# First element of a graph kernel: earlier x, later bias columns, row loads on two queues, weight sums and one row combination moved

## Chip, cores and metric

The kernel runs on one core of one Trainium2 chip. The metric is the device time of one execution in microseconds (us). Lower is better.

## The reference

There are 16 independent elements. Each has node features `x` (1024 x 128) and a dense adjacency matrix `adj` (1024 x 1024), all in float32. An element passes through two stages, each followed by a residual and a layer norm:

```python
# stage 0
degree = adj.sum(-1)[:, :, None]
agg = einsum('bid,bij->bjd', x, adj) / degree
x = layernorm(x + relu(concat([x, agg], -1) @ W.T + b))
# stage 1: four layers
def layer(nodes, adj, ws, bs, wd, bd, wn, bn, wu, bu):
    src = einsum('bjv,bij->biv', nodes @ ws + bs, l2norm(adj, rows))
    dst = einsum('bjv,bji->biv', nodes @ wd + bd, l2norm(adj, columns))
    return tanh(concat([src, nodes @ wn + bn, dst], 2) @ wu + bu)
# layers three and four also see the inputs of earlier layers
x = layernorm(x + layer4(layer3(layer2(layer1(x)))))
```

So each layer multiplies the messages once with the column-normalised adjacency and once with the row-normalised one. These products are nearly all of the work.

## The kernel before

**Tiling.** The 1024 nodes are eight blocks of 128. `a` holds the adjacency of one element in eight blocks of rows (4 MB), `at` its transpose in two halves. Halves of the 1024 columns are written `h` = 0 and 1, and half 1 is worked on first. From layer two on, the two aggregations are done by a seven-product (Winograd) scheme: `y` and `yt` name the four quadrants of `a` and of `at`, `combine_1` overwrites one quadrant by a difference (L672), and `combine(2..4)` build the combinations `T` of `a` and `Q` of `at` (L676, L678, L680; one takes 2.28 us on VectorE). Layer one of the first element is plain (`plain_layer`, L849), because its combinations are not there yet.

**Order.** The order is written out by hand. Each engine executes its instructions in the order of the program text, and a queue issues its DMAs in that order as well. SP (`nc.sync`) carries nearly all DMAs; GpSimd (POOL) issues some at the start. Work of VectorE, ScalarE and GpSimd beside an aggregation is put in by `hooks`: a dictionary from the index of a TensorE step to the function that is called just before that step is issued. Elements after the first have most of their preparation done during the element ahead of them. The first element has no such cover, so it has its own opening, L1045 to L1256.

**The opening.** `load_nodes(q, h)` (L1057) loads half `h` of `x` in four DMAs of 64 KB. `load_pair(q, i, groups)` (L1052) loads two row blocks of the adjacency; SP and POOL carry half of each pair, 256 KB per DMA. `to_xT(h)` transposes a half of `x` on TensorE (L1094) and copies it out on ScalarE (L1095). `weights_of_x(h)` multiplies it by the first half of W (L1179). For each pair, `squares_of` makes the squares of its rows on ScalarE (L1139) and the degrees on VectorE (L1145), and `gathers_of` multiplies `x` by the rows on TensorE (L1152). `add_square(i)` adds the squares of a block into one sum on GpSimd (L1142). `degree_inverses` (L1149) and `degree_row` (L357, L1172) turn the degrees into a row that scales the gathered sums, `scaled` (L1175); then come `weights_of_agT` (L1182), `with_x` (L1190, L1192), the layer norm (L468 to L488) and `to_x1` (L1197). `root_inverses` (L373, L374) takes inverse roots of the sums of squares on VectorE and GpSimd.

**Weights and biases.** `fetch_weights` (L187, L189) loads a layer's weights, `load_biases(i, q)` (L1079) one bias vector per DMA: 9 for i = 0, 8 for i = 1. `bias_columns(i)` transposes them on TensorE (L1084) and copies them on ScalarE (L1085, L1087). `fold_begin` and `fold_end` (L203 to L228) multiply the layers' weight matrices into one. `sums_of_weights` and `weight_sums` (L148 to L155) build the sums of the folded weights that the seven-product scheme needs.

**Rows.** The transpose `at` is made from a second reading of the adjacency by rows, in four groups `rows[0..3]` of 1 MB; a group is eight DMAs of 128 KB (`load_rows_piece`, L638). ScalarE scales them by the row norms (`scale_rows`, L645), VectorE transposes them in blocks of 32 (`transpose_rows`, L653).

Of the kernel before, what the change touches and what calls it, by code (L numbers as in the profile page):

```python
# [14 lines left out]
P = 128  # L15
NL = 4
CHUNKS = [1, 1, 2, 3]
G = 4
# [5 lines left out]
def adj_resnorm_kernel(ctx: ExitStack, tc: tile.TileContext, x, adj, w0, b0, layers, out):  # L24
# [33 lines left out]
    nc = tc.nc  # L58
# [5 lines left out]
    C = P // G  # L64
# [561 lines left out]
    def load_rows(b, q, st):  # L626


        n = QB // len(st)
        for i, piece in enumerate(st):  # L630
            load_rows_piece(b, q, piece, i * n, n)
        return st

    def load_rows_piece(b, q, piece, k, n):
        v = adj[b, q * QB * C:(q + 1) * QB * C].rearrange("(k r) (h g j) -> h g r k j", r=C, h=NH, g=G)
        for g in range(G):
            for h in range(NH):
                nc.sync.dma_start(piece[g * C:(g + 1) * C, :, h * P:(h + 1) * P], v[h, g, :, k:k + n])  # L638
        return piece

    def scale_rows(st, q, rinv, which=range(QB)):
# [424 lines left out]
    for i in range(4):  # L1066
        load_pair(nc.sync, i, (0, 1))
        load_pair(nc.gpsimd, i, (2, 3))
        if i == 1:
            load_nodes(nc.gpsimd, 0)  # L1070
    biases_of = [[b0, *layers[0][1::2], *layers[1][1::2]], [*layers[2][1::2], *layers[3][1::2]]]
    in_rows = one.tile([P, HW], F32, tag="S3", name="biases")
# [4 lines left out]
    def load_biases(i, q, s=slice(None)):  # L1077
        for k, v in list(enumerate(biases_of[i]))[s]:
            q.dma_start(in_rows[k:k + 1, i * P:(i + 1) * P], v.rearrange("(o p) -> o p", o=1))  # L1079
# [11 lines left out]
    def to_xT(h):  # L1091
        pt = small(f"xtr0_{h}", [HW])
        for q in range(BPH):
            nc.tensor.transpose(pt[:, q * P:(q + 1) * P], xn[:, h * BPH + q], ident)  # L1094
        nc.scalar.copy(nodes(xT[:, half(h)]), blocks(pt))  # L1095
# [12 lines left out]
    places[1] = one.tile([P, 2 * NJ, HW // 2], F32, tag="T2", name="rows1_0")  # L1108
    rows, fetched = {}, []
    for l, q in enumerate((None, None, 2, 3)):  # L1110
        if l in (1, 2):
            load_biases(l - 1, nc.sync)
        fetched.append(fetch_weights(raw, l, nc.sync, bcs[l], None if l else wm))
        if q is not None:
            rows[q] = load_rows(0, q, [places[q]])
    wm = as_chunks(wm, 0)
    for q in (0, 1):
        rows[q] = load_rows(0, q, [places[q]])
# [22 lines left out]
    def add_square(i):  # L1141
        nc.gpsimd.tensor_add(sq[4], sq[4], sq[i])  # L1142
# [8 lines left out]
    def gather(h, i):  # L1151
        nc.tensor.matmul(pa[h], xn[:, i], a[:, i, half(h)], start=(i == BPH), stop=(i == BPH - 1))  # L1152

    def squares_of(h, k):
        for i in range(h * BPH + k, h * BPH + k + 2):
            square(i)
            degree(i)
# [19 lines left out]
    def weights_of_x(h):  # L1177
        pw[h] = product(f"pw0_0_{h}")
        nc.tensor.matmul(pw[h], w0T[:, 0], xT[:, half(h)], start=True, stop=False)  # L1179
# [14 lines left out]
    def to_x1(h):  # L1194
# [2 lines left out]
            nc.tensor.transpose(pt[:, q * P:(q + 1) * P], x1n[:, h * BPH + q], ident)  # L1197
        nc.scalar.copy(x1T[:, half(h)], pt)

    weights_of_x(1)  # L1200
    squares_of(*PAIRS[0])
    gathers_of(*PAIRS[0])
    squares_of(*PAIRS[1])
    gathers_of(*PAIRS[1])
    to_xT(0)
    weights_of_x(0)
    nc.vector.tensor_add(sq[6], sq[6], sq[7])
    add_square(5)
    add_square(6)
# [1 line left out]
    degree_row(1)  # L1211
    squares_of(*PAIRS[2])
    gathers_of(*PAIRS[2])
    bias_columns(0)
    add_square(0)
    add_square(1)
    first, second = 2, 3
    nc.scalar.activation(sq[second], a[:, second, :], AF.Copy, accum_out=cols[:, 2 * NB + second:2 * NB + second + 1])
    degree(first)
    gather(1, first)  # L1220
    gather(1, second)
    degree_inverses(0)
    degree_row(0)
    scaled(1)
# [1 line left out]
    weights_of_agT(1)  # L1226
    square(first)
    gather(0, second)
    add_square(first)
    scaled(0)  # L1230
    with_x(1)
    weights_of_agT(0)
# [4 lines left out]
    fold_end(0, fetched[0])  # L1237
    stats[0] = norm_stats(pn[0], range(BPH), "0_0_0")
    root_inverses(cols, inv, slice(NB))
    add_square(second)  # L1240
    biases = fold_begin(1, fetched[1], nc.vector.tensor_copy, True)
    for q in range(BPH):
# [18 lines left out]
    for b in range(B):  # L1261
# [8 lines left out]
        if b == 0:  # L1270
            def row_factors0():
                column_sums(0, st0)
                for q in (2, 3):
                    scale_rows(rows[q], q, rinv)

            def second_x1():
                to_x1(0)
                bias_columns(1)
                fold_begin(2, fetched[2])
                ahead["spread"] = row_inverses(0, inv)  # L1280

            def factors_and_fold():
                nonlocal rinv
                fold_end(2, fetched[2])
                rinv = gather_inverses(0, ahead["spread"])

            ahead = {}
            t = messages(b, 0, feats, wm, {0: second_x1, 1: factors_and_fold, 2: row_factors0}, with_sums=False)
            cinv = {}

            def columns0(rows, h, engine=nc.vector):
                scale_columns(a, cinv[0], rows, half(h), engine)

            def rows0(destination, finish):
                for q in (2, 3):
                    transpose_rows(rows[q], q, at)
                sums_of_weights(2, fetched[2][3])
                weight_sums(own_seven(2, fetched[2][3]))
                nc.sync.dma_start(wsave[2], fetched[2][3])

            def cinv0(destination, finish):
                cinv[0] = factor_rows_now(0, 1, inv, "cinv")

            def second0(destination, finish):
                columns0(range(NJ, NB), 1)
                destination(1, cinv[0])
                columns0(range(NJ), 1)

            def fold_and_scale(l, q):
                fold_begin(l, fetched[l])  # L1310
                scale_rows(rows[q], q, rinv)

            def first0(destination, finish):
                columns0(range(NJ, NB), 0, nc.gpsimd)
                columns0(range(2), 0, nc.gpsimd)
                for q in (0, 1):
                    transpose_rows(rows[q], q, at)
                destination(0, cinv[0])
                columns0(range(2, NJ), 0)

            def sums0(destination, finish):
                combine_1(y)
                finish(1)
                combine(2, y, T)
                combine_1(yt)
                combine(3, y, T)

            def folded(l, part):
                return lambda *_: part(l, fetched[l])

            hooks = {4: lambda *_: inverses(0, st0, NB), 6: rows0, 7: cinv0,
                     9: lambda *_: fold_and_scale(3, 0), 11: second0, 12: folded(3, fold_end),
                     14: lambda *_: scale_rows(rows[1], 1, rinv), 18: first0, 26: sums0}
            T = combined(0, "T")
            plain_layer(b, 0, feats, t, wm, a, at, f1, "acc", hooks)
            wm = message_weights(b, 1)
            a2 = load(n)
            xs2 = load_spread(n)
        else:
            w = {}  # L1340
            if nxt:
                st = begin_sums(n)
            t = messages(b, 0, feats, wm)
            if nxt:
                w["a"] = load(n)
            Q = combined(b, "Q")
            ahead = {}

            def weights1(ahead=ahead):
                combine(4, y, T)  # L1350
                ahead["wm"] = message_weights(b, 1)

            def rows3():
                transpose_rows(rows[0], 0, at)

            def sums1(w=w, st=st):
                if nxt:
                    for i in range(2):
                        squares_of_row(n, w["a"], st, i)

            def additions(*which, then=(), w=w, st=st):
                def issue():
                    if nxt:
                        for i in which:
                            add_squares(n, st, i)
                        for i in then:
                            squares_of_row(n, w["a"], st, i)
                return issue

            hooks = {0: rows3, 3: weights1, 5: lambda: combine_1(yt), 7: lambda: combine(2, yt, Q),  # L1370
                     9: lambda: combine(3, yt, Q), 15: sums1, 16: additions(1), 17: lambda: combine(4, yt, Q),
                     18: additions(then=(2, 3)), 23: additions(2), 27: additions(3)}
            aggregate(b, 0, feats, t, wm, a, at, T, Q, f1, "row", hooks)
            wm = ahead["wm"]
            a2, xs2 = w.get("a"), None
# [20 lines left out]

        hooks = {}
        if b == 0:
            hooks = {0: sums_of(0, 1, add=(1,)), 1: lambda: combine(2, yt, Q), 2: sums_of(of=FIRST),
                     3: sums_of(2, 3, add=(2, 3)), 4: lambda: combine(3, yt, Q), 5: sums_of(4, 5, add=(4, 5)),  # L1400
                     6: lambda: combine(4, y, T), 13: sums_of(6, 7), 18: lambda: combine(4, yt, Q), 19: sums_of(of=LAST),
                     22: sums_of(add=(6, 7)), 27: lambda: column_sums(n, st)}
            st = begin_sums(n)
        else:
# [284 lines left out]
```

## Time and profile before

| | us |
|---|---|
| median of three runs | 2397.73 |
| lowest and highest run | 2396.9, 2400.73 |
| time of the profiled execution | 2395.86 |
| its span, first to last instruction | 2394.1 |
| TensorE busy in the span | 2377.4 |
| TensorE busy in 0 to 10, 10 to 20, 20 to 30 | 6.22, 9.21, 9.20 |
| TensorE busy in 80 to 85, in 85 to 110, in 110 to 130 | 3.76, 25.0, 17.79 |

The engines are PE (TensorE products), PEld (TensorE weight loads), DVE (VectorE), ACT (ScalarE), POOL (GpSimd) and SP (the queue of DMAs). L12 is a line of the kernel. A row of a timeline has the start, the duration, the engine, the line, the operation, what it writes and reads, and in brackets the idle time of the engine ahead of it with what ended it. A product in float32 appears as two matrix instructions.

### The profile page before, as it was taken

Reading aid. Unit: us, or ns where it says so; the run is one execution under the profiler, and the core shown is the slowest. Engines: PE = TensorE matmul, PEld = TensorE weight load, DVE = VectorE, ACT = ScalarE, POOL = GpSimd, SP = SyncE. Lnnn points to the kernel's source line nnn. Section 1 sums busy time; section 2 is a strip of 40 time slices with the busy share of each in tenths; the row PEclk is TensorE's granted clock in tenths of the full one; section 3 lists DMA queues with packets and bytes.
Section 4 is the critical chain, followed back from the end, with each engine's and each line's share of the span. In section 5 each row is a group of like instructions: output and inputs, shape, how many; then the busy total and the mean of one; then the engine's idle time right before and its main releaser. Section 6 shows DMA issues by size and latency. Waiting matters only on the chain.

```text
span 2394.1 us, 39329 instructions
## 1 busy us (share of the span) xinstructions
PE 2377.4 (99%) x15289; PEld 1279.6 (53%) x15289; DVE 2092.6 (87%) x2817; ACT 980.8 (41%) x1845; POOL 275.8 (12%) x103
## 2 busy tenths in 40 slices
PE   8999999999999999999999999999999999999998
PEld 4444564645556455554655546456464554645555
DVE  6998888999889989889988889888898988998954
ACT  5425345253343524435244452434525344352322
POOL 4101111001111011110111110111100111101110
PEclk9999999999999999999999999999999999999999
DMA  9527244262533627335272442634427253362400
GB/s 205 124 75 147 69 115 90 70 148 57 135 78 81 138 48 157 61 97 115 55 163 55 108 97 71 147 69 110 91 70 151 57 133 76 80 141 48 100 22 22
DMA packets 363387, 232.03 MB, mean 97 GB/s; under 512 B 150353, under 2 KB 334306, under 8 KB 363202
## 3 DMA queue, kind: packets, MB, share of 16 engines
q1 hardware_dynamic: 362386, 227.03, 42.5%
q0 software_dynamic: 816, 2.49, 0.4%
q8 instruction: 121, 1.98, 0.4%
q14 instruction: 64, 0.52, 0.1%
HBM read 209.59 MB, written 19.84 MB: 96 GB/s over the span
## 4 chain that ended last, share of the span: by engine, by line
PE 92%; DVE 1%; issue 0%; POOLq 0%; ACT 0%; DVEq 0%
PE m L1003 40%; PE z L1003 28%; PE pt L245 9%; PE pt_z L245 5%; PE m_f L581 5%; PE z_f L581 2%; PE pw L245 2%; PE m3s L1003 1%; PE pt_p L245 1%; DVE t L752 0%; PE pv L250 0%; PE pm L250 0%; DVE f L534 0%; PE rp L250 0%; DVE t L758 0%
## 5 line engine op out<-in xcount | busy, mean ns | idle before, releaser
L1003 PE MATMUL m<-a,t 128*64 128x512 f32 x1008 | 434.7, 593 | 0.2 <-DVE t L709 0.2
L1003 PE MATMUL m<-at,t 128*64 128x512 f32 x1008 | 418.6, 592 | 0.0
L1003 PE MATMUL m<-Q,S 128*64 128x512 f32 x880 | 394.0, 593 | 0.0
L1003 PE MATMUL m<-T,S 128*64 128x512 f32 (+1 forms) x1040 | 393.6, 573 | 0.0
L454 POOL TENSOR_TENSOR rs<-ve,mhalf 128x32 f32<-128x32 f32 x30 | 191.9, 6396 | 988.4 <-DVE ve L452 988.4
L1003 PE MATMUL z<-at,t 128*64 128x512 f32 x504 | 229.2, 592 | 0.0
L1003 PE MATMUL z<-at,S 128*64 128x512 f32 x504 | 228.3, 593 | 0.0
L1003 PE MATMUL z<-a,S 128*64 128x512 f32 x504 | 228.2, 593 | 0.0
L1003 PE MATMUL z<-a,t 128*64 128x512 f32 x504 | 227.2, 593 | 0.0
L1003 PE MATMUL z<-Q,t 128*64 128x512 f32 x504 | 227.0, 593 | 0.0
L1003 PEld LDWEIGHTS m<-T,S 128*64 128x64 f32 x1040 | 131.3, 137 | 129.5 <-issue 127.6
L1003 PEld LDWEIGHTS m<-Q,S 128*64 128x64 f32 x880 | 118.2, 137 | 150.4 <-issue 143.0
L1003 PEld LDWEIGHTS m<-at,t 128*64 128x64 f32 x1008 | 131.6, 137 | 110.7 <-issue 109.4
L1003 PEld LDWEIGHTS m<-a,t 128*64 128x64 f32 x1008 | 132.0, 137 | 109.8 <-issue 101.0
L1003 PE MATMUL z<-T,t 128*64 128x512 f32 x384 | 172.8, 592 | 0.0
L882 ACT COPY e<-m 64x512 f32<-64x512 f32 x63 | 36.7, 582 | 327.4 <-PE m L1003 327.0
L374 POOL TENSOR_TENSOR inv<-cols,mhalf 128x16 f32<-128x16 f32 (+1 forms) x17 | 46.8, 2751 | 1033.3 <-DVE cols L373 1033.3
L412 DVE TENSOR_TENSOR a<-a,cinv 128x512 f32<-128x512 f32 x250 | 155.6, 696 | 0.8 <-DMA xn<-in_x_dram 0.8
L320 ACT ACTIVATE sq<-a 128x1024 f32<-128x1024 f32 x120 | 125.9, 1050 | 37.0 <-DVE acc L327 23.1
L245 PE MATMUL pt<-wm,f1T 128*64 128x128 f32 (+1 forms) x1536 | 134.3, 309 | 1.2 <-ACT f1T L1021 1.2
L245 PEld LDWEIGHTS pt<-wm,f1T 128*64 128x64 f32 x1536 | 109.1, 137 | 34.6 <-issue 12.3
L315 ACT ACTIVATE a<-a 128x1024 f32<-128x1024 f32 x120 | 125.3, 1045 | 0.4
(309 smaller groups left out, 5023.3 us busy)
## 6 DMA issues: line engine op xcount, KB each, us to landing
a<-in_adj_dram SPq DMA_DIRECT2D x120, 512.0 KB
rows<-in_adj_dram SPq DMA_DIRECT2D x480, 64.0 KB
a<-in_adj_dram SPq DMA_DIRECT2D x240, 128.0 KB
wm<-wsave SPq DMA_DIRECT2D x32, 704.0 KB
wm<-wsave SPq DMA_DIRECT2D x31, 320.0 KB
xn<-in_x_dram SPq DMA_DIRECT2D x124, 64.0 KB
xs<-in_x_dram SPq DMA_DIRECT2D x60, 128.0 KB
cinv<-dr SPq DMA_DIRECT2D x30, 256.0 KB
```

The costliest lines, as they stand in the source:

```text
L245: nc.tensor.matmul(out[s], x[:, s], y, start=start, stop=stop)
L315: nc.scalar.activation(a[:, i, :], a[:, i, :], AF.Copy, accum_out=degree)
L320: nc.scalar.activation(sq, a[:, i, :], AF.Square, accum_out=state["cols"][:, i:i + 1])
L374: nc.gpsimd.tensor_tensor(inv[:, s], cols[:, s], mhalf[:, s], ALU.pow)
L412: engine.tensor_mul(a[:, i, s], a[:, i, s], cinv[:, s])
L454: nc.gpsimd.tensor_tensor(rstd, ve, mhalf[:, :n], ALU.pow)
L581: nc.tensor.matmul(o, x_, y_, start=start, stop=stop)
L882: nc.scalar.copy(e0[high], A[high])
L1003: nc.tensor.matmul(o, x, y_, start=start, stop=stop)
```

## The change

All of it is in the first element.

- The other half of `x` (four DMAs on POOL) is issued after pair 0 and no longer after pair 1. `to_xT(0)` and `weights_of_x(0)` stand ahead of all squares and gathers.
- `load_biases(1)` is issued after layer three's weights and half of row group 2. `bias_columns(0)` stands after the first two gathers of the last pair.
- Row groups 2 and 3: SP loads partition groups 0 and 1 where it loaded all four, and POOL loads groups 2 and 3, after `add_square(1)`.
- `add_square(first)` (block 2) stands after `root_inverses`.
- `sums_of_weights(2)` moves from hook 6 of layer one to hook 4, ahead of `inverses`.
- `combine_1(yt)` moves from hook 26 of layer one to hook 1 of layer two, ahead of `combine(2, yt, Q)`. `combine(4, y, T)` moves from hook 6 of layer two to hook 4.

```diff
-    def load_rows_piece(b, q, piece, k, n):
+    def load_rows_piece(b, q, piece, k, n, groups=range(G), engine=nc.sync):
...
-        for g in range(G):
+        for g in groups:
             for h in range(NH):
-                nc.sync.dma_start(piece[g * C:(g + 1) * C, :, h * P:(h + 1) * P], v[h, g, :, k:k + n])
+                engine.dma_start(piece[g * C:(g + 1) * C, :, h * P:(h + 1) * P], v[h, g, :, k:k + n])
...
         load_pair(nc.gpsimd, i, (2, 3))
-        if i == 1:
+        if i == 0:
             load_nodes(nc.gpsimd, 0)
...
-        if l in (1, 2):
-            load_biases(l - 1, nc.sync)
+        if l == 1:
+            load_biases(0, nc.sync)
         fetched.append(fetch_weights(raw, l, nc.sync, bcs[l], None if l else wm))
         if q is not None:
-            rows[q] = load_rows(0, q, [places[q]])
+            rows[q] = [load_rows_piece(0, q, places[q], 0, QB, (0, 1))]
+        if l == 2:
+            load_biases(1, nc.sync)
...
+    to_xT(0)
     weights_of_x(1)
+    weights_of_x(0)
     squares_of(*PAIRS[0])
...
     gathers_of(*PAIRS[1])
-    to_xT(0)
-    weights_of_x(0)
...
     gathers_of(*PAIRS[2])
-    bias_columns(0)
     add_square(0)
     add_square(1)
+    for q in (2, 3):
+        load_rows_piece(0, q, places[q], 0, QB, (2, 3), nc.gpsimd)
...
     gather(1, second)
+    bias_columns(0)
     degree_inverses(0)
...
     gather(0, second)
-    add_square(first)
     scaled(0)
...
     root_inverses(cols, inv, slice(NB))
+    add_square(first)
     add_square(second)
...
             def rows0(destination, finish):
                 for q in (2, 3):
                     transpose_rows(rows[q], q, at)
-                sums_of_weights(2, fetched[2][3])
                 weight_sums(own_seven(2, fetched[2][3]))
...
                 combine(2, y, T)
-                combine_1(yt)
                 combine(3, y, T)
...
-            hooks = {4: lambda *_: inverses(0, st0, NB), 6: rows0, 7: cinv0,
+            def inverses0(destination, finish):
+                sums_of_weights(2, fetched[2][3])
+                inverses(0, st0, NB)
+
+            hooks = {4: inverses0, 6: rows0, 7: cinv0,
...
-            hooks = {0: sums_of(0, 1, add=(1,)), 1: lambda: combine(2, yt, Q), 2: sums_of(of=FIRST),
-                     3: sums_of(2, 3, add=(2, 3)), 4: lambda: combine(3, yt, Q), 5: sums_of(4, 5, add=(4, 5)),
-                     6: lambda: combine(4, y, T), 13: sums_of(6, 7), 18: lambda: combine(4, yt, Q), 19: sums_of(of=LAST),
+            def third_of_rows(y=y, yt=yt, T=T, Q=Q):
+                combine(3, yt, Q)
+                combine(4, y, T)
+
+            def first_of_rows(yt=yt, Q=Q):
+                combine_1(yt)
+                combine(2, yt, Q)
+
+            hooks = {0: sums_of(0, 1, add=(1,)), 1: first_of_rows, 2: sums_of(of=FIRST),
+                     3: sums_of(2, 3, add=(2, 3)), 4: third_of_rows, 5: sums_of(4, 5, add=(4, 5)),
+                     13: sums_of(6, 7), 18: lambda: combine(4, yt, Q), 19: sums_of(of=LAST),
```

## The prediction

> **What bounds the kernel now.** I read the page first, then the waits of TensorE, then the timelines of the first 130 us, because the diff touches the first of the 16 elements alone.
>
> ```profile
> PE 2377.4 (99%) x15289; PEld 1279.6 (53%) x15289; DVE 2092.6 (87%) x2817; ACT 980.8 (41%) x1845; POOL 275.8 (12%) x103
> ```
>
> TensorE is idle for 16.7 us of 2394.1, so nothing here can win more than some of that. The waits of TensorE over the first 300 us name where it is lost (engine, line, releaser: us, times, longest):
>
> ```profile
> PE pa L1152 <- DMA a<-in_adj_dram: 1.6, 1, 1.6
> PE pt L245 <- ACT f1T L1021: 1.2, 1, 1.2
> PE pt L245 <- DVE e L719: 1.2, 1, 1.2
> PE pt L245 <- DVE e L761: 1.0, 1, 1.0
> PE biases L1084 <- DMA biases<-in_L_gnn_bu_dram: 0.7, 1, 0.7
> PE pw L1179 <- ACT x_T L1095: 0.7, 1, 0.7
> ```
>
> The 1.6, the two 0.7 and the first 1.2 are what the change aims at; the other two, at the entry of layer three, are VectorE's. TensorE's timeline at the start (start, us, what, wait) shows the order of the work before the change:
>
> ```profile
> 7.15 1.12 PE L1179 MATMUL pw<-x_T,w0T 128*128 128x512 f32 x2 [0.73 <-ACT w0T L1104]
> 9.86 7.45 PE L1152 MATMUL pa<-a,xn 128*128 128x512 f32 x16 [1.59 <-DMA a<-in_adj_dram]
> 17.15 0.60 PE L1094 MATMUL xtr<-ident,xn 128*128 128x128 f32 x4
> 18.43 1.12 PE L1179 MATMUL pw<-x_T,w0T 128*128 128x512 f32 x2 [0.68 <-ACT x_T L1095]
> 19.39 0.60 PE L357 MATMUL dinv<-ident,inv 128*128 128x128 f32 x4
> 19.83 3.60 PE L1152 MATMUL pa<-a,xn 128*128 128x512 f32 x8
> 24.12 0.20 PE L1084 MATMUL biases<-ident,biases 9*128 9x9 f32 x1 [0.69 <-DMA biases<-in_L_gnn_bu_dram]
> 24.29 1.96 PE L1152 MATMUL pa<-a,xn 128*128 128x512 f32 x4
> ```
>
> A 128x512 product is two passes 0.43 us apart (16 passes in 6.9 us). From 9.86 to 24.29 TensorE is nearly full: the last adjacency pair has landed at 21.5 (VectorE's degree begins at 21.51 on that DMA), but TensorE reaches it at 24.29. So this stage is bound by TensorE's order, not by the transfer.
>
> VectorE's timeline around the end of layer one, and where it next holds TensorE:
>
> ```profile
> 77.04 2.28 DVE L672 TENSOR_TENSOR at<-at,at 128x2048 f32<-128x2048 f32 x1
> 79.24 2.28 DVE L678 TENSOR_TENSOR T<-T,a 128x2048 f32<-128x2048 f32 x1
> 81.44 0.68 DVE L843 TENSOR_TENSOR e<-e,z 128x512 f32<-128x512 f32 x1
> ...
> 103.99 2.29 DVE L680 TENSOR_TENSOR Q<-at,Q 128x2048 f32<-128x2048 f32 x1
> ...
> 113.73 0.68 DVE L719 TENSOR_TENSOR e<-f23T,f1T 128x512 f32<-128x512 f32 x1
> ```
>
> L843 needs layer one's last product (issued until 79.75), but stands behind L672 and L678; hence the 1.2 on f1T. From the last message addition to L719 VectorE stops for only 0.68 and 0.47 us, both for a ScalarE copy of its own result.
>
> **What the Trainium skill says.** "TensorE: Matmul & The Clock Gate", Part 1: the clock falls to half after about one idle window of 3.4 us, rises after a busy one, and the windows run free. The trace agrees on both sides: the three idle products at 1.46 start their passes 0.85 us apart until about 4.6, 0.43 after; at the end the last product runs out at 2387.86 and the granted clock, 1.00 until 2390.0, is 0.50 from 2390.5. "DMA: Bandwidth & Descriptors", Issuing engines are not separate DMA queues: a second issuing queue saves issue time only. Here the row transfers run at 190 to 260 GB/s whoever issues, so I credit no bandwidth. "SBUF — State Buffer", Who interferes with whom: a VectorE operation with two SBUF inputs and a GpSimd one that reads SBUF exclude each other. The trace agrees: L379, 0.18 us elsewhere, took 1.78 at 38.63 and ended at 40.41, as GpSimd's addition (38.01 to 40.36) ended.
>
> **The change part by part**, in us against the profiled execution.
>
> *x's rest first; TensorE waits for it.* GpSimd's queue now issues W, two adjacency pieces, four of x, then the rest. By the DMA view of single issues, the first two adjacency pieces land at 6.3 and 8.9, the next at 10.8 and 12.6, then x at 13.6 to 15.3, 0.6 apart. Moved behind the second piece, x's last lands at 8.9 + 4 x 0.6 = 11.3, or 11.6 with the 1.0 its first took. L1094 for half 0 now precedes L1179 and all gathers, so TensorE stands from 6.4 to 11.5 (range 10.8 to 11.7), and behind it the ScalarE copy and the squares. Then: four transposes 0.5, two L1179 products 1.7, 24 gather passes and the degree transposes 24 x 0.43 + 0.4 = 10.7: the last pair begins at 24.4. Pair one, now behind x, lands at 15.1 and is wanted at 17.1. Before: 24.29. The bias transposes come 1.9 later, after their landing at 24.1, so the wait goes but 0.2 of work stays: the degree transposes start at 26.4 for 26.08. **+0.3** (-0.4 to +0.6). The saved waits pay for the pause and no more. add_square(2) moved later lies on GpSimd, whose next product, L477, is needed only after 32.6; bias columns on ScalarE precede yT's use of them by 1 us.
>
> *The pause cools the clock.* It is 5.1 us against 1.6 now. A window that held 0.9 us of work was enough to lower the clock at the end; a 5.1 us pause leaves at most 0.9 us of work in some window whatever the phase. Half speed until a busy window has passed, 3.4 us in the likeliest phase, delays work that has no slack by half of it: **+1.6** (0 to +3.4).
>
> *Rows by two queues; biases later.* SP sheds 8 of its 16 row issues ahead of rows 0 and 1, of 0.34 to 0.5 each, and moves 8 bias issues (2.4) past rows 2; GpSimd gains 8 issues of 0.55 = 4.4, about 28 to 33, between L1142 and L477. Rows 3 now hold ScalarE 1.5 us at 48.28, and TensorE not at all. The biases land by about 36 and are wanted at 38.5. **0**; if GpSimd's issue ran a microsecond over, L477 and the centring behind it would lose that (0 to +1), and the first moved addition stands behind it too. The two additions now back to back behind L374 (2.35 each) can hold L379 until 43; its reader on TensorE comes at 42.93: **+0.1** (0 to +0.5).
>
> *Weight sums in a pause.* Five operations, 54.14 to 55.49, move to 47.87, where VectorE waits until 48.91. They take 1.35 of 1.04, so L366, GpSimd's power behind it and the transposes of cinv come 0.4 later; those start at 51.47 with TensorE full and the power done at 51.28. **+0.4** (0 to +0.5). The 1.35 saved later is slack there.
>
> *combine_1(yt) moves to layer two.* L843 then starts as its product ends, near 80, and f1T is there when TensorE wants it: **-1.2**. But the 2.2 us (pitch of L672) go into the stretch up to L719, which has no slack: **+2.2** (+1.0 to +2.3). On the way the fourth combination of the rows (L680), finished at 106.27 for a use at 107.03, is late, and TensorE waits 1.5 there; L719's wait then takes the rest.
>
> **Sum:** 0.3 + 1.6 + 0.1 + 0.4 - 1.2 + 2.2 = **+3.4**, 0.14%. L761's wait stays; after it TensorE waits 0.3 at most, so nothing gives it back. The profiled execution took 2395.86; it would take 2399.3. The median of the runs shown is 2397.73, 1.9 above it, so I expect **2401.1**. About 0.2% (4.8 us: below 2392.9 or above 2402.5) is what a measurement of this kernel can tell from no change.
>
> **Rivals.** (a) TensorE's clock does not fall: 3.4 - 1.6 = +1.8, 2399.5. For it: the page of the clock record starts at 1.00 and shows nothing of the start, and the first pause may be judged otherwise. Against: the fall at 2390. (b) Slower: the half clock lasts two windows, because work begins inside one and only a fully busy one counts. At the start the window was some 92% busy, which allows this. The loss is 3.4 instead of 1.6: +5.2, 2402.9. It decides from 6 us of half clock on, counted from the first transpose at 11.5. (c) x lands before the first adjacency pair is whole (9.86) and VectorE's stretch has room. Then TensorE sheds 3.0 us before 24.29, but is held at 21.5 by the last pair and at 24.1 by the biases, so the degree transposes gain 1.8; with -1.2 and +0.4 that is -2.6, 2395.1. Against: GpSimd's second piece lands at 8.9 and x stands behind it. (d) The change does not do what it says: x lands no earlier than now (15.3), since the queues share the engines. TensorE would start 3.8 later still and the sum be +7; the landings in issue order speak against it.
>
> **Numbers.** My forecast 0.45, (a) 0.20, (b) 0.22, (c) 0.11, (d) 0.02. The range 2396.0 to 2404.0 holds the forecast, (a), (b) and the upper end of (c). Faster by over 0.2%: 0.03, since even (c) reaches only 0.11%. Slower: (b), (d) and the forecast's upper tail, less (b)'s lower part: 0.27. Within: 0.70.
>
> **What would show it.** L1094's second group at about 11.5 with L1152 behind it near 13.7 or later, its first passes 0.85 apart and a clock below 1.00 in 10 to 15; the last gathers near 26; no wait on f1T near 80; a wait on L680 of about 1.5 and L719 some 3.4 later than 113.73. Gathers beginning before 11, or L719 earlier than now, would prove me wrong.

## The result and the profile after

The changed kernel takes **2402.16 us** (median; 2401.29 to 2402.99) against 2396.60 for the kernel before (2395.49 to 2401.11 in the same measurement). The ratio is 1.0021, with a 95% interval of 1.0013 to 1.0028: 5.6 us slower. Its profiled execution took 2402.39, with a span of 2400.6. That span is 6.5 longer than the one of before (2394.1), and the profiles below account for these 6.5.

The busy row of the page of the changed kernel:

```profile
PE 2380.8 (99%) x15289; PEld 1283.5 (53%) x15289; DVE 2091.9 (87%) x2817; ACT 980.1 (41%) x1845; POOL 279.3 (12%) x111
```

The number of matrix instructions is the same, yet TensorE is busy for 3.4 us longer (2377.4 before) and idle for 19.8 instead of 16.7. So there is more waiting, and the same instructions take longer; below, the record of the granted clock shows why. Both have to be found.

TensorE's waits over the first 300 us (releaser: us, times, longest):

```profile
PE xtr L1094 <- DMA xn<-in_x_dram: 7.0, 1, 7.0
PE z L1003 <- DVE Q L680: 2.5, 1, 2.5
...
PE pt L245 <- DVE e L761: 1.0, 1, 1.0
...
PE pt L245 <- DVE e L719: 0.2, 1, 0.2
```

All that the change aimed at is gone from this view: the waits on the adjacency, on the biases, on `x_T` and on f1T. Two new ones stand in their place, 7.0 and 2.5. TensorE's timeline of the opening (start, us, what, wait; the added lines have moved L1152 to L1154 and L1179 to L1181):

```profile
5.89 0.60 PE L1094 MATMUL xtr<-ident,xn 128*128 128x128 f32 x4
6.32 0.38 PE L1103 MATMUL w0tr<-ident,w0n 128*128 128x128 f32 x2
13.69 1.09 PE L1094 MATMUL xtr<-ident,xn 128*128 128x128 f32 x4 [6.98 <-DMA xn<-in_x_dram]
14.57 3.62 PE L1181 MATMUL pw<-x_T,w0T 128*128 128x512 f32 x4
17.98 7.38 PE L1154 MATMUL pa<-a,xn 128*128 128x512 f32 x16
25.20 0.60 PE L357 MATMUL dinv<-ident,inv 128*128 128x128 f32 x4
25.63 5.32 PE L1154 MATMUL pa<-a,xn 128*128 128x512 f32 x12
...
31.04 0.65 PE L357 MATMUL dinv<-ident,inv 128*128 128x128 f32 x4
```

The four transposes of `x` that took 0.60 at 5.89 take 1.09 at 13.69: same instruction, other clock. The second group of degree transposes (L357), which ends the opening, starts at 31.04. In the kernel before it started at 26.08:

```profile
26.08 0.60 PE L357 MATMUL dinv<-ident,inv 128*128 128x128 f32 x4
```

The windows of the same stretch of the changed kernel (us, busy time of PE, PEld, DVE, ACT, POOL with counts, then the granted clock, the DMA share and GB/s):

```profile
11.00:11.50 0.50, 0.00 (x0) 0.00 (x0) 0.50 (x1) 0.00 (x0) 0.00 (x0) 1.00 0.98 221
11.50:12.00 0.50, 0.00 (x0) 0.00 (x0) 0.50 (x1) 0.00 (x0) 0.40 (x1) 0.84 1.12 287
12.00:15.00 3.00, 1.31 (x5) 1.25 (x6) 1.23 (x2) 0.19 (x1) 0.77 (x3) 0.50 1.03 309
15.00:18.00 3.00, 3.00 (x5) 1.00 (x4) 1.09 (x1) 3.00 (x6) 0.44 (x1) 0.50 1.03 313
...
18.50:19.00 0.50, 0.50 (x2) 0.19 (x1) 0.50 (x1) 0.50 (x2) 0.50 (x1) 0.83 1.15 335
```

A mean of 0.84 over half a microsecond is 0.16 us at half clock, so the clock fell at 11.84. Likewise 0.83 in the last row means that it rose at 18.67. Half clock lasted 6.83 us, and TensorE worked through the last 5.0 of them (13.69 to 18.67).

VectorE's timeline at the end of layer one and up to L719, the addition that layer three waits for:

```profile
84.95 0.69 DVE L843 TENSOR_TENSOR e<-e,z 128x512 f32<-128x512 f32 x1 [1.65 <-PE z L849]
...
102.48 2.28 DVE L680 TENSOR_TENSOR T<-a,T 128x2048 f32<-128x2048 f32 x1
104.68 2.55 DVE L329 TENSOR_TENSOR acc<-acc,sq 128x1024 f32<-128x1024 f32 x2
...
110.28 0.69 DVE L908 TENSOR_TENSOR e<-e,e 64x512 f32<-64x512 f32 x1 [1.73 <-ACT e L891]
111.00 2.29 DVE L680 TENSOR_TENSOR Q<-at,Q 128x2048 f32<-128x2048 f32 x1
...
120.75 0.68 DVE L719 TENSOR_TENSOR e<-f23T,f1T 128x512 f32<-128x512 f32 x1
```

L843 now waits for TensorE (1.65) and no longer the other way round. But from L843 to L680 on `Q` it takes 26.05 us where it took 22.55.

**A ledger.** Five milestones cut the run into stretches that can be compared between kernels: the second L357 of the opening (A), the first product of layer one (L849, B), L843 at its end (C), L680 on `Q` (D) and L719 (E). All numbers are differences of starts in the profiles; the last two columns are E to the end of the span, and the span.

| kernel | A | A to B | B to C | C to D | D to E | E to end | span |
|---|---|---|---|---|---|---|---|
| before | 26.08 | 18.84 | 36.52 | 22.55 | 9.74 | 2280.4 | 2394.1 |
| after | 31.04 | 18.82 | 35.09 | 26.05 | 9.75 | 2279.9 | 2400.6 |
| e1 x back | 26.27 | 19.38 | 35.10 | 26.04 | 9.75 | 2280.1 | 2396.6 |
| e2 combinations back | 30.79 | 18.82 | 35.45 | 22.55 | 9.74 | 2279.9 | 2397.2 |
| e3 pause filled | 29.65 | 18.82 | 35.10 | 26.05 | 9.74 | 2279.9 | 2399.3 |
| e4 load order alone | 29.68 | 18.82 | 35.10 | 26.05 | 9.75 | 2279.7 | 2399.1 |
| e5 x and combinations back | 26.00 | 18.81 | 35.45 | 22.55 | 9.75 | 2280.0 | 2392.6 |
| e6 rows on one queue | 31.38 | 18.82 | 35.10 | 26.04 | 9.74 | 2279.8 | 2400.9 |
| e7 fourth one back | 31.40 | 18.82 | 35.10 | 25.00 | 9.75 | 2280.3 | 2400.4 |
| e8 sums alone | 26.08 | 18.85 | 35.44 | 22.54 | 9.76 | 2280.1 | 2392.8 |
| e9 sums, biases later | 27.41 | 18.90 | 35.44 | 22.54 | 9.75 | 2280.2 | 2394.2 |
| e10 combinations alone | 25.66 | 18.83 | 34.93 | 26.05 | 9.75 | 2280.0 | 2395.2 |

Three of the columns are all but constant, so the whole change is in A, B to C and C to D. Between before and after they move by +4.96, -1.43 and +3.50, together **+7.0**; the remaining stretches take 0.5 off it (a wait of 0.27 at L583 goes, among others), and the span is 6.5 longer. Column A also varies where the opening is the same. Where `x` is early and read first (after, e2, e6, e7), it is 30.79 to 31.40. The landing does not explain that: x's transposes start within 0.40 us of each other (13.51 to 13.91), and the latest of these starts has the earliest A. The clock explains it, as the last section shows. Where x's part is as in the kernel before, A is 25.66 to 27.41; the first gathers start at 9.28 (e10) to 10.69 (e9) there, and e9 also ran at half clock from 12.06 to 15.47.

### The profile page after: what moved, and what is told of

Read it like the earlier page. It is cut to its first block, busy times and chain, and to the rows that moved or that the text cites. A ratio compares the mean times of both kernels' runs of the same rounds, so it can differ in the third digit from the quotient of the medians.

```text
span 2400.6 us, 39327 instructions
## 1 busy us (share of the span) xinstructions
PE 2380.8 (99%) x15289; PEld 1283.5 (53%) x15289; DVE 2091.9 (87%) x2817; ACT 980.1 (41%) x1845; POOL 279.3 (12%) x111
## 4 chain that ended last, share of the span: by engine, by line
PE 94%; DMA 2%; DVE 2%; ACT 1%; issue 0%; SPq 0%; POOLq 0%; DVEq 0%; ACTq 0%
PE m L1003 40%; PE z L1003 28%; PE pt L245 9%; PE pt_z L245 5%; PE m_f L581 5%; PE z_f L581 2%; PE pw L245 2%; DMA Q<-in_adj_dram 1%; PE m3s L1003 1%; DMA wm<-in_L_gnn_ws_dram 1%; PE z L849 1%; PE pt_p L245 1%; DVE acc L329 0%; DMA a<-in_adj_dram 0%; DMA rows<-in_adj_dram 0%
## 5 line engine op out<-in xcount | busy, mean ns | idle before, releaser
L412 DVE TENSOR_TENSOR a<-a,cinv 128x512 f32<-128x512 f32 x250 | 153.8, 696 | 0.3 <-DMA xn<-in_x_dram 0.3
```

What stands on the lines that cost most here:

```text
L412: engine.tensor_mul(a[:, i, s], a[:, i, s], cinv[:, s])
```

## The experiments

The theory after the result: the opening is late because TensorE now stands until `x` has landed and then works at half clock, and layer two is late because of the moved combination. The rivals: TensorE's order is at fault and not the order of the loads, the clock costs little, the combination's move pays for itself, or the rows on two queues take their part. Medians, and ratios to the kernel before with their 95% intervals (before had 2396.35 beside the first four, 2396.55 beside e5 and e7 to e9, 2396.07 beside e10 and e6; the change itself had 2396.60, so before's own median moved by up to 0.5 between measurements):

| kernel | median us | ratio | interval |
|---|---|---|---|
| e1 x back | 2397.68 | 1.0006 | 0.9997 to 1.0014 |
| e2 combinations back | 2399.01 | 1.0010 | 1.0004 to 1.0017 |
| e3 pause filled | 2400.68 | 1.0017 | 1.0009 to 1.0024 |
| e4 load order alone | 2400.97 | 1.0020 | 1.0012 to 1.0027 |
| e5 x and combinations back | 2394.80 | 0.9992 | 0.9984 to 1.0000 |
| e6 rows on one queue | 2402.19 | 1.0024 | 1.0015 to 1.0034 |
| e7 fourth one back | 2400.89 | 1.0018 | 1.0011 to 1.0026 |
| e8 sums alone | 2395.39 | 0.9995 | 0.9986 to 1.0003 |
| e9 sums, biases later | 2394.88 | 0.9993 | 0.9985 to 1.0001 |
| e10 combinations alone | 2398.21 | 1.0010 | 1.0002 to 1.0019 |

**e1: x's part undone**, all else as in the change.

```diff
-        if i == 0:
+        if i == 1:
             load_nodes(nc.gpsimd, 0)
...
-    to_xT(0)
     weights_of_x(1)
-    weights_of_x(0)
...
     gathers_of(*PAIRS[1])
+    to_xT(0)
+    weights_of_x(0)
```

> The changed kernel with x's other half loaded and worked on where it was before (behind pair 1 in GpSimd's queue; its transposes and product behind the gathers of pair 1). All other edits stay. Theory (the opening costs 5, the combination in layer two 2): no wait of 7.0 on x, clock 1.00 from 10 to 20, the degree transposes of half 0 at about 25.4 instead of 31.0 (0.7 earlier than before the change, because the bias wait is gone), L719 still some 1.3 later than before (the 2.0 of layer two less that 0.7); the time about 5.6 below the changed kernel. Rival (row issues on GpSimd or the later biases cost the time): the degree transposes come back to 25.4, but the messages and layer one start no earlier than some 3 us behind before, and the time stays near the changed kernel's.

Measured: 4.5 us below the changed kernel where 5.6 was expected, no wait on `x`, the clock at 1.00 throughout, and A back at 26.27 (25.4 expected; the first gathers start at 10.52 for 9.86 before). So x's part is worth some 4.5 to 5. The median is still 1.3 above before, which the interval does not tell from nothing, but the ledger shows the 3.5 from C to D in full. Three waits of TensorE in e1:

```profile
PE z L1003 <- DVE Q L680: 2.5, 1, 2.5
...
PE pt L245 <- DVE e L719: 1.9, 1, 1.9
...
PE biases L1084 <- DMA raw<-in_L_gnn_ws_dram: 0.9, 1, 0.9
```

The last one, on the second group of bias columns, is the 0.55 of e1 from A to B; it stands in no other kernel of the ledger. These biases are the ones that the change loads later.

**e2: the two combinations put back** (`combine_1(yt)` into layer one, `combine(4, y, T)` to hook 6), all else as in the change.

```diff
                 combine(2, y, T)
+                combine_1(yt)
                 combine(3, y, T)
...
-            hooks = {0: sums_of(0, 1, add=(1,)), 1: first_of_rows, 2: sums_of(of=FIRST),
-                     3: sums_of(2, 3, add=(2, 3)), 4: third_of_rows, 5: sums_of(4, 5, add=(4, 5)),
+            hooks = {0: sums_of(0, 1, add=(1,)), 1: lambda: combine(2, yt, Q), 2: sums_of(of=FIRST),
+                     3: sums_of(2, 3, add=(2, 3)), 4: lambda: combine(3, yt, Q), 5: sums_of(4, 5, add=(4, 5)),
+                     6: lambda: combine(4, y, T),
```

> The changed kernel with combine_1(yt) in layer one and combine(4, y, T) at hook 6 of layer two, as before. Theory: the wait of 1.2 on f1T comes back, the wait of 2.5 on L680 and the second stretch at half clock behind it go, L719 starts at about 118.8 instead of 120.75, and the time falls by 2.0. Rival (the move won its 1.2 and the late L719 comes from the opening alone): L719 stays 7 later than before and the time rises by 1.2.

Measured: 3.1 us below the changed kernel, more than the 2.0 expected. C to D is 22.55 again, and the wait on L680 is gone. Half clock in layer two did not go with it: it now comes behind the wait of 1.2 on L719, from 120.35 to 123.77, and E to the end is still 2279.9. The wait on f1T did not come back, though the prediction had put its end down to this move. L843 of e2 on VectorE:

```profile
85.06 0.68 DVE L843 TENSOR_TENSOR e<-e,z 128x512 f32<-128x512 f32 x1
```

It has no wait ahead of it, follows the combination at once, and is in time all the same. So something else in the change had already cleared the way for it.

**e8: only the weight sums moved**, from hook 6 to hook 4 of layer one, in the kernel before.

```diff
                 for q in (2, 3):
                     transpose_rows(rows[q], q, at)
-                sums_of_weights(2, fetched[2][3])
...
+            def inverses0(destination, finish):
+                sums_of_weights(2, fetched[2][3])
+                inverses(0, st0, NB)
...
-            hooks = {4: lambda *_: inverses(0, st0, NB), 6: rows0, 7: cinv0,
+            hooks = {4: inverses0, 6: rows0, 7: cinv0,
```

> The kernel before with the weight sums of layer three moved to hook 4 alone. Theory (this edit, not the combination's move, frees L843): the wait of 1.2 on f1T is gone or below 0.3, cinv's transposes come 0.1 to 0.4 later, L719 comes 1.1 earlier than before at the same opening, the time 1.0 below before. Rival (f1T comes in time by the earlier rows or by the move): the wait on f1T stays near 1.2 and the time is within 0.3.

Measured: the f1T wait is gone, with the combination where it always was. B to C is 1.08 shorter, C to D unchanged, and the median is 1.2 below its before, though its interval reaches 1.0003. VectorE in e8:

```profile
80.37 0.68 DVE L843 TENSOR_TENSOR e<-e,z 128x512 f32<-128x512 f32 x1
...
102.91 2.29 DVE L680 TENSOR_TENSOR Q<-at,Q 128x2048 f32<-128x2048 f32 x1
...
112.67 0.68 DVE L719 TENSOR_TENSOR e<-f23T,f1T 128x512 f32<-128x512 f32 x1
```

L719 is 1.06 earlier than before's 113.73 with A in the same place. The cost that was feared, a later `cinvp`, is 0.1 (51.59 for 51.47). On the way VectorE gained more than the 1.35 that was moved: it reaches the first combination of layer one (L672 on `a`) at 69.14 for 72.03, because the eight scalings of `a` ahead of it (L412) also took 6.8 instead of 8.7. Why they are shorter no run tests. Only 1.08 of this counts, since the first L843 then waits 1.72 for TensorE.

**e10: only the combinations moved**, in the kernel before (the hooks of the change, the sums where they were).

```diff
                 combine(2, y, T)
-                combine_1(yt)
                 combine(3, y, T)
...
-            hooks = {0: sums_of(0, 1, add=(1,)), 1: lambda: combine(2, yt, Q), 2: sums_of(of=FIRST),
-                     3: sums_of(2, 3, add=(2, 3)), 4: lambda: combine(3, yt, Q), 5: sums_of(4, 5, add=(4, 5)),
-                     6: lambda: combine(4, y, T), 13: sums_of(6, 7), 18: lambda: combine(4, yt, Q), 19: sums_of(of=LAST),
...
+            hooks = {0: sums_of(0, 1, add=(1,)), 1: first_of_rows, 2: sums_of(of=FIRST),
+                     3: sums_of(2, 3, add=(2, 3)), 4: third_of_rows, 5: sums_of(4, 5, add=(4, 5)),
+                     13: sums_of(6, 7), 18: lambda: combine(4, yt, Q), 19: sums_of(of=LAST),
```

> The kernel before, with the two combinations of the rows moved as in the change (the first one to hook 1 of layer two, the fourth one of the columns to hook 4) and nothing else. Theory: whichever work of VectorE is taken from ahead of the self-term addition (L843) at the end of layer one, the wait on f1T of 1.2 us goes; but the combination's 2.2 us and the later ScalarE squares come back ahead of the addition that layer three waits for. So: no wait on f1T, a wait on the fourth combination (L680) of some 2.5 us, that addition (L719) about 3.2 - 1.1 = 2.0 us later than in the kernel before at the same opening, median 1.3 to 2.3 us above the kernel before. Rival (the prediction's own steps): 2.2 - 1.2 = +1.0, with a wait on L680 of 1.5. Rival (the combination's move is free without the rest of the change): the median within 0.4 us of the kernel before, no wait on L680 above 0.7.

Measured: 2.1 us above its before. B to C falls by 1.59, C to D rises by 3.50, so E comes 1.9 later against the same opening. TensorE's wait in e10:

```profile
PE z L1003 <- DVE Q L680: 2.5, 1, 2.5
```

Together with e8 this settles the f1T wait: either edit alone removes all of it. Beside the moved sums, the combination's move takes another 0.35 from B to C (35.44 in e8, 35.09 in the changed kernel). Beside the moved combination, the moved sums take nothing more (34.93 in e10, 35.09 with both). So the gain can be booked to either edit, but only once. The sums have it for nothing, the combination costs 3.5 from C to D; beside the sums, those 3.5 buy 0.35.

**e7: only `combine(4, y, T)` back at hook 6**, in the changed kernel, behind the squares of blocks 4 and 5.

```diff
                 combine(3, yt, Q)
-                combine(4, y, T)
...
                      3: sums_of(2, 3, add=(2, 3)), 4: third_of_rows, 5: sums_of(4, 5, add=(4, 5)),
+                     6: lambda: combine(4, y, T),
```

> The changed kernel with combine(4, y, T) back at hook 6 of layer two, behind the additions of squares 4 and 5; combine_1(yt) stays in layer two. Theory (the move costs 2.2 of VectorE's work, and 1.0 more because ScalarE, which waits with squares 6 and 7 for those additions to free a buffer, comes late with L891): L908 waits 0.7 instead of 1.7, L680 ends 1.0 earlier, TensorE's wait on it is 1.5 instead of 2.5, too short for the clock to fall, and L719 comes 1.0 earlier; the time 0.5 to 1.0 below the changed kernel. Rival (VectorE alone): nothing moves.

The reason for this run is ScalarE's timeline in the changed kernel:

```profile
105.93 1.06 ACT L320 ACTIVATE sq<-a 128x1024 f32<-128x1024 f32 x1 [2.58 <-DVE acc L329]
...
107.26 1.06 ACT L320 ACTIVATE sq<-a 128x1024 f32<-128x1024 f32 x1 [0.18 <-DVE acc L329]
...
108.43 0.58 ACT L886 COPY e<-m 64x512 f32<-64x512 f32 x1
109.02 0.58 ACT L887 COPY e<-m 64x512 f32<-64x512 f32 x1
109.63 0.62 ACT L891 COPY e<-e 64x512 f32<-64x512 f32 x1
```

`squares_of_row` has two buffers. With the fourth combination at hook 4, VectorE adds the squares (L329) only from 104.68, after it; ScalarE waits 2.58 for a free buffer, and the copies behind it (L886 to L891) are late for VectorE's L908, which stands for 1.73. Measured in e7, on VectorE:

```profile
109.60 0.69 DVE L908 TENSOR_TENSOR e<-e,e 64x512 f32<-64x512 f32 x1 [0.68 <-ACT e L891]
110.32 2.29 DVE L680 TENSOR_TENSOR Q<-at,Q 128x2048 f32<-128x2048 f32 x1
```

The wait is 0.68 as in the kernel before (L908 at 103.27 there), C to D is 25.00, and the median 1.3 below the changed kernel (0.5 to 1.0 expected). TensorE's wait on L680 is 1.4. So the 3.50 are 2.45 for the combination's work and 1.05 for the round trip through ScalarE.

**e3: the pause filled** with eight products of `idle` ahead of x's transposes; nothing else differs from the changed kernel.

```diff
+    pt = product("warm")
+    for _ in range(8):
+        nc.tensor.matmul(pt, idle[:, :P], idle, start=True, stop=True)
     to_xT(0)
     weights_of_x(1)
     weights_of_x(0)
```

> The changed kernel with eight more products on the zeroed tile ahead of x's transposes of half 0, so that TensorE works in its pause; their result is not used. Theory (half of the opening's loss is the clock): x lands where it did, the clock is 1.00 throughout, the gathers' passes are 0.43 apart at once, the degree transposes of half 0 come at 28.6 instead of 31.0 and the time falls by 2.4. Rival (the loss is the late start alone, and what follows is bound by the landing of the pairs): the clock is full and the degree transposes still come near 31.

TensorE's timeline in e3:

```profile
7.84 7.03 PE L1204 MATMUL warm<-idle 128*128 128x512 f32 x16
14.71 0.60 PE L1094 MATMUL xtr<-ident,xn 128*128 128x128 f32 x4
15.14 1.96 PE L1181 MATMUL pw<-x_T,w0T 128*128 128x512 f32 x4
16.95 7.03 PE L1154 MATMUL pa<-a,xn 128*128 128x512 f32 x16
...
29.65 0.65 PE L357 MATMUL dinv<-ident,inv 128*128 128x128 f32 x4
```

The transposes take 0.60 again, and from them to A it takes 14.94 (14.71 to 29.65) where the changed kernel needs 17.35 (13.69 to 31.04). The difference, **2.41 us, is the price of the clock alone** in the changed kernel's execution. The median is 1.5 below the changed kernel and not 2.4; the filling kept TensorE until 14.71, 1.0 past the 13.69 at which x's transposes start in the changed kernel, and A is 1.4 earlier. It fills the pause and does not remove it: A is still 3.6 later than before.

**e4: the load order alone**, with TensorE's order put back as in e1 and `x` still loaded after pair 0.

> The changed kernel with x's half loaded early as changed, but its transposes and product behind the gathers of pair 1 as before. Theory: the gathers of pair 0 start near 9.9, but pair 1 now stands behind x in GpSimd's queue and lands at about 17 instead of 13.6, so TensorE waits some 3.5 there, with the clock perhaps at half again; the degree transposes of half 0 at 28 to 30, the time 1 to 3 below the changed kernel: the load order alone costs. Rival (only TensorE's order costs, the loads are neutral): the degree transposes at 25.4, as without the edit.

TensorE's timeline in e4:

```profile
10.09 3.67 PE L1154 MATMUL pa<-a,xn 128*128 128x512 f32 x8 [1.04 <-DMA a<-in_adj_dram]
16.52 5.25 PE L1154 MATMUL pa<-a,xn 128*128 128x512 f32 x8 [2.75 <-DMA a<-in_adj_dram]
...
29.68 0.65 PE L357 MATMUL dinv<-ident,inv 128*128 128x128 f32 x4
```

TensorE has the first pair at 10.09, about as in the kernel before (9.86), but pair 1, now behind `x` in GpSimd's queue, costs a wait of 2.75 and then some half clock (5.25 for 3.67). A is 29.68, 3.4 later than in e1, and the median is 1.2 below the changed kernel (1 to 3 expected). So most of the loss is already in the order of the loads; TensorE's order adds 1.4 to A (31.04).

**e5: x and both combinations back**, the rest of the change kept (e1's and e2's edits together).

> The changed kernel with both x's part and the combinations put back as before: what stays is the later biases, the rows by two queues, the moved addition and the weight sums in the pause. Theory (the loss is x's part and the combinations, the rest gains a little): the opening ends within 0.7 of before, no wait on f1T, as in the run with the combination back, L719 about 0.4 later to 1.0 earlier than before, the time within 1 of before. A wait of 0.9 on bias_columns(1), seen where x's part alone was put back, may come again; without it the time is 1 below before. Rival (something in this rest costs too): L719 over 1.5 later than before.

Measured: 2394.80, 7.4 below the changed kernel. What is left is the sums' gain. The kernel is 1.75 below before, with an interval that ends at 1.0000, just about the limit of what can be told apart. It has the lowest ratio of the ten, with e9 and e8 close to it; if any version beats the kernel before, it is these.

**e9: sums moved and `bias_columns(0)` later**, in the kernel before (e8's edit and the next one).

```diff
     gathers_of(*PAIRS[2])
-    bias_columns(0)
...
     gather(1, second)
+    bias_columns(0)
```

> The kernel before with the weight sums at hook 4 and bias_columns(0) behind the first two gathers of the last pair; loads, rows and combinations as before. Theory: the wait of 0.7 on the biases goes, the degree transposes of half 0 come at 25.4 to 25.6 instead of 26.08, and with the sums the time is 1.6 below before. Rival (the last pair's landing holds the gathers): the degree transposes stay near 26.

Measured: 2394.88, 0.5 below e8, less than these intervals separate. Its profiled execution had a late landing (first gathers at 10.69), half clock behind it (12.06 to 15.47), and so A at 27.41 where 25.4 to 25.6 was expected; the biases' wait is gone from it. Whether the later biases bring anything stays open.

**e6: all rows on SP again**, all else as in the changed kernel.

```diff
-            rows[q] = [load_rows_piece(0, q, places[q], 0, QB, (0, 1))]
+            rows[q] = load_rows(0, q, [places[q]])
...
-    for q in (2, 3):
-        load_rows_piece(0, q, places[q], 0, QB, (2, 3), nc.gpsimd)
```

> The changed kernel with all of row groups 2 and 3 loaded by SP again. Theory: the second queue brings and costs nothing here, because the rows are wanted later than they land either way: within 0.8 us of the changed kernel, the first message product and L719 within 0.5 us of it. Rival (GpSimd's eight issues of 0.58 us, 4.7 us in all, hold up L477 and the centring behind it): 0.7 us or more faster than the changed kernel and the wait on GpSimd around the first layer norm gone. Rival (two queues spread the load): 1 us or more slower, with the ScalarE scaling of row groups 2 and 3 and what TensorE transposes behind it later.

Measured: 2402.19, the changed kernel's time, and every stretch from A to E the same to 0.01. The second queue for the rows brings and costs nothing here.

## Why the prediction was right or wrong

The direction was right and the forecast of 2401.1 lay 1.1 below the measured median, but that is closer than its steps were, and in part luck. The sum was +3.4 against the profiled execution; the profile shows +6.5. It came near because the step from the profile to the median (1.9, from three runs) was itself too large: in the larger measurement before's median stands 0.7 above its profile, and after's 0.2 below. The prediction's largest chance, 0.70, lay on a change of less than 0.2%. The measured one is 0.21%, with an interval from 0.13% to 0.28%, too near to that border to tell.

- **What bounds the kernel: right for the kernel before.** TensorE is full, the opening is bound by its order, and the end is set by L719 in all twelve kernels (E to the end is 2280.0 within 0.4). After the change the opening is bound by x's landing and the clock.
- **x's landing: too early by 2.2.** The step said 8.9 + 4 x 0.6 = 11.3, or 11.6, and took 11.5. TensorE got the last piece at 13.69. GpSimd's timeline, whose own issues wait for earlier landings of its queue, shows where the time went:

```profile
6.86 0.53 POOL L1055 DMA_DIRECT2D a<-in_adj_dram  x1 [0.31 <-DMA a<-in_adj_dram]
9.91 0.53 POOL L1055 DMA_DIRECT2D a<-in_adj_dram  x1 [2.52 <-DMA a<-in_adj_dram]
11.60 0.53 POOL L1055 DMA_DIRECT2D a<-in_adj_dram  x1 [1.17 <-DMA xn<-in_x_dram]
12.68 0.53 POOL L1055 DMA_DIRECT2D a<-in_adj_dram  x1 [0.55 <-DMA xn<-in_x_dram]
```

  The second adjacency piece landed at 9.9 and not 8.9, and the four of `x` took 3.8 after it and not 2.4 to 2.7. A pace read in one place of a queue was carried to another one, with other transfers under way beside it. What slowed it there no run shows.
- **The order after the landing: right.** From x's transposes to A the prediction counted 14.9 (11.5 to 26.4). e3, at full clock, shows 14.94.
- **The clock: rival (b)'s mechanism, not the forecast's.** The half clock lasted two windows and not one: the window in which the work began did not raise it. It was 6.83 us in all, of which work saw only the last 5.0, so it cost 2.4: between the forecast's 1.6 and the rival's 3.4. The rival's deciding figure, 6 us from the first transpose, took it for granted that work and half clock begin together; in the changed kernel the clock fell 1.85 ahead of it. How much of the half clock meets work depends on the execution: 4.04 us in e2 and 6.06 in e7, with the same opening.
- **Sums in a pause: wrong sign.** The step said +0.4 at `cinvp` and called the 1.35 saved later slack. It cost 0.1, and the 1.35 were not slack: they lie on VectorE ahead of L843, whose lateness the prediction had itself read as the f1T wait. That gain (1.1) was then booked to the combination.
- **The combination: mis-sized, and booked a gain that the sums already had.** -1.2 + 2.2 = +1.0 was predicted. Alone it is +1.9 (e10), and beside the moved sums +3.15 (3.50 less 0.35). The 2.2 of work was nearly right (2.45). The missing 1.05 is the fourth combination's move to hook 4, which the prediction did not price at all: it holds up ScalarE through the two square buffers. The wait on L680 was 2.5 and not 1.5 for that reason (1.4 in e7).
- **Rows on two queues, biases later, moved addition: right at about 0.** A to B is 18.82 for 18.84, so even the +0.1 for L379 did not show. e6 confirms it for the rows. The later biases cost 0.55 in one execution, that of e1.
- **Rivals (c) and (d).** `x` came neither ahead of the first pair nor as late as before (15.3); both are out.

Step by step, at E: opening 4.96 for the predicted 1.9 (landing 2.2 and clock 0.8 more), sums -1.1 for +0.4, combinations (counted after the sums) +3.15 for +1.0, L379 0 for 0.1. The sum is 7.0 for 3.4.

## What to carry to other kernels

When several edits aim at one wait, ask what each leaves for the others: here either of two edits removed the wait on f1T, one for nothing and the other by moving 2.2 us of work into a full stretch. When work is moved past the producer of a buffered operand, follow the buffer to the other engine as well. And before an operand is read first in program order, ask what happens if it lands two microseconds late: everything behind it waits, and here the clock that fell in the pause cost 2.4 of the opening's 5.0.

## What was not expected of the hardware

**The clock's windows.** The Trainium skill, "TensorE: Matmul & The Clock Gate", Part 1, has the clock rise after a busy window of about 3.4 us and fall after an idle one. The runs agree on the length: in each trace the changes of the clock lie a whole number of 3.41 us apart. Half clock lasted 6.83 us in the opening and, in the changed kernel's layer two, from 114.24 to 117.66, 3.42 (two windows and one). What counts as busy or idle is finer, and there the measurement decides. The window that ended at 15.25 (11.84 + 3.41) held 1.56 us of work (13.69 to 15.25), 46%, and did not raise the clock. In e6 half clock lasted three windows, from about 9.2 to 19.5:

```profile
9.00:10.00 1.00, 0.00 (x0) 0.00 (x0) 0.00 (x0) 0.00 (x0) 0.00 (x1) 0.61 1.09 217
...
19.00:20.00 1.00, 1.00 (x3) 0.30 (x3) 0.51 (x1) 0.46 (x2) 0.82 (x1) 0.77 1.07 227
```

The second of the three held 2.47 us of work (13.58 to 16.05), 72%, and did not raise the clock either. The window that ended at 114.24 held 0.90 (from 113.34), 26%, and lowered it; in e9 one with about 1.4 (10.69 to 12.06), 41%, did so too. If the first 260 us of all twelve traces are cut into such windows, they part almost cleanly. At full clock, every window with up to 41% of work was followed by half clock and every one from 47% on by full clock; of five at 44 or 45% one was followed by half clock. At half clock, every window with up to 81% was followed by half clock and every one from 83% on by full clock. These are shares of TensorE's busy time in the profile, products and transposes alike; the record of the clock begins with its first rise, and ahead of that half clock is read from passes some 0.85 us apart. So one pause of 2.5 us can be enough, and the phase decides: the same wait of 2.5 on L680 lowered the clock in the changed kernel at once and in e3 not at all.

**The price of half clock.** It is half of the time that full work spends in it, and nothing for the part that falls into the pause. Four executions have the same opening, and e3 took 14.94 from x's transposes to A at full clock (all in us):

| kernel | x's transposes | half clock | of it with work | transposes to A | more than e3 |
|---|---|---|---|---|---|
| after | 13.69 | 11.84 to 18.67 | 4.98 | 17.35 | 2.41 |
| e2 | 13.91 | 11.13 to 17.95 | 4.04 | 16.88 | 1.94 |
| e6 | 13.58 | 9.23 to 19.47 | 5.89 | 17.80 | 2.86 |
| e7 | 13.51 | 9.33 to 19.57 | 6.06 | 17.89 | 2.95 |

In each row the last number is half of the time with work, within 0.1. This is the spread of column A.

**A slow clock off the path cost nothing here.** In the changed kernel TensorE ran at half clock from 114.24 to 117.66. Yet D to E is 9.75 there and 9.74 in e3, which stayed at full clock, because L719 is VectorE's. The slow passes only used up TensorE's wait ahead of L719, 0.17 for 1.9 in e3.
